# Moving two places for other work in the third layer's attention loop, and two edits around the first layer's experts

## The chip, the cores and the metric

The kernel runs on one core of a Trainium2 chip. The metric is the device time of one execution, in microseconds (us); lower is better. A core has five engines, each with its own queue of instructions that it works off in order: TensorE (matrix products and transposes; PE in the profile, with its weight loads as PEld), VectorE (DVE), ScalarE (ACT), GpSimd (POOL) and SyncE (SP, which issues most of the transfers). They wait for one another by semaphores. TensorE writes its results to PSUM, a small memory of eight banks of 128 x 512 numbers; VectorE and ScalarE read them from there into SBUF, where everything else lies.

## The reference, cut to what matters

The input is x, 8 batches of 512 tokens of 128 numbers. Four layers follow each other, and each is a sandwich: half a feed-forward block, an attention, and the same half feed-forward block again, each on a normalised x:

```python
x = x + 0.5 * _L0_ffn_ref(_layernorm(x), ...)      # 8 experts of capacity 512, top 2; the eighth is a no-op
x = x + _L0_attn_ref(_layernorm(x), ...)           # 16 heads in segments of 32 tokens
x = x + 0.5 * _L0_ffn_ref(_layernorm(x), ...)
x = x + 0.5 * _L1_ffn_ref(...); x = x + _L1_attn_ref(...); x = x + 0.5 * _L1_ffn_ref(...)
x = x + 0.5 * _L2_ffn_ref(...); x = x + _L2_attn_ref(...); x = x + 0.5 * _L2_ffn_ref(...)
x = x + 0.5 * _L3_ffn_ref(...); x = x + _L3_attn_ref(...); x = x + 0.5 * _L3_ffn_ref(...)
```

(The normalisation stands ahead of every block of every layer.) The change touches layer 0's feed-forward blocks and layer 2's attention. The latter, called L2 here, is causal, with 16 heads of 64 and a slope for the distance of two tokens:

```python
q = (x @ Wq).reshape(b, n, H, DH); k = ...; v = ...
scores = einsum('bihd,bjhd->bhij', q, k) * scale + slope * (pos_i - pos_j), masked to j <= i
out = einsum('bhij,bjhd->bihd', softmax(scores), v).reshape(b, n, H * DH) @ Wo + bo
```

The feed-forward block of layer 1 routes a token to one of 64 small splines by two stages of gates (an exponential, a table of knots, a first maximum) and scales a direction by the spline's value. That of layer 2 is one product with a weighted sum of 8 matrices. That of layer 3 adds the products of the 2 best of 8 experts.

## The kernel before, in words

x stays in SBUF, as eight tiles of 128 x 4 x 128 (one a batch). The work runs layer by layer, but a batch's feed-forward blocks of the layers next to an attention are cut into small steps and put between the attention's own work.

**Layer 0's experts** (function `experts`, lines 656 to 710) run twice. A table in DRAM, xd, holds the normalised tokens. For each of seven experts GpSimd gathers 512 rows by four indirect transfers (`fetch`, L664), TensorE turns them (`turn`, L676), multiplies them with the first matrix in four pieces (`inner`, L684, tiles hp), which ScalarE and VectorE take out of PSUM in turn (L688, L686), and with the second (`outer`, L694); ScalarE scales the result (y, L697), and GpSimd writes it out by four indirect transfers (`put`, L668) to a table yd that must hold zeros where no expert writes. There are two such tables, one for each run; `zeros(n)` (L464) fills table n by four transfers of 1 MB from a tile z of zeros. The list `beside` holds small works that are spread over the seven experts, in the place `k * 7 // len(beside)`: in the first run the zeros of the second table, eight `self_part` (the no-op expert's share of a batch, VectorE, L654), and the loads of layer 1's weights. In the second run eight `self_part`, eight `multiply` (the products up x down of layer 3's experts, L1912, in one PSUM bank f3, with loads two ahead, L1905), nine `add` (layer 2's summed matrix, VectorE, L1675; the ninth its bias, L1681) take turns. After each run the rows are read back (L482, tiles r) and added.

**The loop of L2** (lines 1857 to 1891) goes over 64 units, a unit n being a pair of heads of one batch (eight units a batch). The order in which TensorE, ScalarE and VectorE get their instructions is exactly that of the code (`manual_schedule`); GpSimd and SP are ordered by a scheduler. Scores are made in four stretches of queries, i = 0 to 3, of width 128 to 512. `score` (L1753) makes one stretch for both heads of the pair in a PSUM tile s of two banks (two of these tiles); VectorE adds the slopes and finds the minimum in one custom instruction (L1757, the "reduction"); ScalarE takes the exponential (L1760), whose call `score` hands back so that the loop can place it. `norm` (L1787, L1790) divides by the sums. `turn(n, m)` transposes four of the 128 x 128 blocks of the result into one bank (L1779) and hands back ScalarE's copy pt (L1781); five turns, m = 4, 0, 1, 2, 3, make a unit. `project` (L1721, copies qk L1723) makes the queries and keys of a unit, `values` (L1734) half the values of two, `weigh` (L1804, copy att L1807) the weighted values, and `leave` (L1813) the output product of a batch. Turns, projections, values, weighted values and all steps from outside take their PSUM banks from four, tag "mm"; which bank a tile gets is settled when the program is built, by which comes free. In unit n TensorE's order is: three turns of n - 1 (4, 0, 1), the projections of n + 1, scores 2 and 1 of n, turns 2 and 3 of n - 1, values, weighing of n - 2, scores 3 and 0 of n + 1. The exponentials of scores 3 and 0 are kept (`late`) and run at the head of the next unit, between the copies of its first turns.

**The places for other work.** `todo` maps a number to a list of works, and `works(at)` (L1848) runs that list. A unit has three places, 3n, 3n + 1, 3n + 2. In the repeating stretch a batch puts into them, among others:

- layer 2's update: a turned block (L314), then `update` (L348, VectorE L351), in a first and a second place;
- layer 1's front: `scores` and `squeeze` (sp L1048, ScalarE's copy L1049, a gelu L1055 with its table load, VectorE L1054) in a second place, together with an update, and `finish` (VectorE L1060 and L1061, ScalarE's tanh L1063) in the third place after it;
- layer 1's sixteen steps: nearly all on VectorE; `turn` in a first place, `spline` (pa L1138 of 130 columns, ScalarE's copy L1145, eight VectorE steps L1148 to L1155) in the second place, `direct` (pa L1138 of 256 columns, four ScalarE activations L1163 scaled by the spline's result) in the third place after it;
- layer 3's steps: a turned block in a second place, `route` (lp L366, VectorE L416 and L417, ScalarE's exponential L321) in the third place after it, and eight `apply` (yp L384, four VectorE instructions L386) in eight places that follow each other, so in first, second and third ones. The second of the eight shares its place with `direct`.

At the end of the stretch layer 3's first steps come in: a turned block (L314, copy xta L321) in a third place and the first projection (L1979) in a second.

Of the kernel before, what the change touches and what calls it, by code (L numbers as in the profile page):

```python
# [8 lines left out]
F32 = mybir.dt.float32  # L9
# [7 lines left out]
P = 128  # L17
NB = 8
# [126 lines left out]
class Net:  # L145
# [316 lines left out]
        return w  # L462

    def zeros(self, n):  # L464
        for k in range(4):
            self.nc.sync.dma_start(
                out=self.yds[n][2048 * k : 2048 * k + 2048, :].rearrange("(p n) d -> p (n d)", p=P), in_=self.z)
# [24 lines left out]
    def l0_block(self, w):  # L492
# [8 lines left out]
        with ExitStack() as c:  # L501
# [149 lines left out]
            def self_part(b):  # L651
                for i in range(4):
                    t, x = 4 * b + i, self.x[b][:, i, :]
                    nc.vector.scalar_tensor_tensor(x, self.xn[b][:, i, :], box["pw"][:, t, 7:8], x, ALU.mult, ALU.add)  # L654

            def experts(wk, ps, n, beside):

                src, dst, yd = box["src"], box["dst"], self.yds[n]
                gs, gts, hs, ys = {}, {}, {}, {}

                def fetch(e, s):
                    if s == 0:
                        gs[e] = wk.tile([P, 4, P + 8], F32, tag="g", name="g", bufs=4)
                    nc.gpsimd.indirect_dma_start(  # L664
                        out=gs[e][:, s, :], out_offset=None, in_=self.xd[:, :], in_offset=bass.IndirectOffsetOnAxis(ap=src[:, e, s : s + 1], axis=0))

                def put(e, s):
                    put = nc.gpsimd.indirect_dma_start(  # L668
                        out=yd[:, :], out_offset=bass.IndirectOffsetOnAxis(ap=dst[:, e, s : s + 1], axis=0), in_=ys[e][:, s, :], in_offset=None)

                    self.apart(f"puts{n}", put.ins)

                def turn(e):
                    gp = ps.tile([P, 512], F32, tag="mm", name="gp")
                    for s in range(4):
                        nc.tensor.transpose(gp[:, s * P : (s + 1) * P], gs[e][:, s, 0:P], self.ident)  # L676
                    gts[e] = wk.tile([P, 512], F32, tag="gt", name="gt")
                    nc.vector.tensor_copy(gts[e], gp)

                def inner(e):  # L680
                    h = hs[e] = wk.tile([P, 4, 512], F32, tag="h", name="h")
                    for ic in range(4):
                        hp = ps.tile([P, 512], F32, tag="hp", name="hp")
                        nc.tensor.matmul(hp, lhsT=w["w1"][:, e, ic * P : (ic + 1) * P], rhs=gts[e], start=True, stop=True)  # L684
                        if ic % 2:
                            nc.vector.tensor_scalar(h[:, ic, :], hp, 0.0, None, ALU.max)  # L686
                        else:
                            nc.scalar.activation(h[:, ic, :], hp, AF.Relu)  # L688

                def outer(e):  # L690
                    op = ps.tile([P, 4, P], F32, tag="mm", name="op")
                    for s in range(4):
                        for ic in range(4):
                            nc.tensor.matmul(op[:, s, :], lhsT=hs[e][:, ic, s * P : (s + 1) * P], rhs=w["w2"][:, e, ic, :], start=(ic == 0), stop=(ic == 3))  # L694
                    y = ys[e] = wk.tile([P, 4, P], F32, tag="y", name="y", bufs=3)
                    for s in range(4):
                        nc.scalar.activation(y[:, s, :], op[:, s, :], AF.Copy, scale=gs[e][:, s, P + e : P + e + 1])  # L697

                for e in range(3):
                    for s in range(4):  # L700
                        fetch(e, s)
                turn(0)
                for e in range(7):
                    inner(e)
                    if e < 6:
                        turn(e + 1)
                    outer(e)
                    for s in range(4):
                        put(e, s)
                        if e + 3 < 7:  # L710
                            fetch(e + 3, s)
                    for k, work in enumerate(beside):
                        if k * 7 // len(beside) == e:
                            work()
# [171 lines left out]
                slots(bank)  # L886
            with tc.tile_pool(name="f0w", bufs=2) as wk, tc.tile_pool(name="f0e", bufs=2, space=PSUM) as ps, ordered(engines={*FIXED, mybir.EngineType.SP}):
                more = [lambda: box.__setitem__("w1", self.l1_ffn_weights(self.keep))]
                experts(wk, ps, 0, [lambda: self.zeros(1)] + [lambda b=b: self_part(b) for b in range(NB)] + more)
            with tc.tile_pool(name="f0m", bufs=2) as wk, tc.tile_pool(name="f0c", bufs=7, space=PSUM) as ps, ordered(engines=every):  # L890
                todo, bank = {}, banks(ps)
                load, both, add = self.returned(wk, self.yds[0], 3, True)
# [1 line left out]
                for g in range(4):  # L894
                    n = PACE * g
                    for k in range(2):
                        b = 2 * g + k
# [9 lines left out]
            with tc.tile_pool(name="f0w", bufs=2) as wk, tc.tile_pool(name="f0e", bufs=2, space=PSUM) as ps, ordered(engines=FIXED):  # L907
                w2, more = box["w2"]
                w3, steps = self.l3_ffn_weights(self.keep, wk, ps)
                parts = [lambda b=b: self_part(b) for b in range(NB)]  # L910
                experts(wk, ps, 1, [work for works in zip(parts, steps, more(ps)) for work in works] + [more(ps)[8]])
        return box["w1"], w2, w3

    def apart(self, group, ins):
# [774 lines left out]
    def l2_block(self, w1, w2, w3, xt0):  # L1689
# [13 lines left out]
        with ExitStack() as c:  # L1703
            pool = c.enter_context(tc.tile_pool(name="a2", bufs=1))
            wk = c.enter_context(tc.tile_pool(name="a2w", bufs=2))
# [62 lines left out]
            def turn(n, m):  # L1768


                if m == 4:
                    blocks = [(jj, i, 2) for jj in range(2) for i in (2, 3)]
                else:
                    blocks = [(m // 2, i, 1) for i in (1, 2, 3)] + [(m // 2, 3, 3)] if m % 2 else [(m // 2, i, 0) for i in range(4)]
                if n not in turned:
                    turned[n] = wk.tile([P, 5, 512], F32, tag="pt", name="pt")
                tp = bank("tp", (P, 4, P))
                for k, (jj, i, kt) in enumerate(blocks):
                    nc.tensor.transpose(tp[:, k, :], block(n, jj, i, kt), self.ident)  # L1779
                to = turned[n][:, m, :].rearrange("p (k q) -> p k q", q=P)  # L1780
                return lambda: nc.scalar.copy(to, tp)  # L1781
# [35 lines left out]
            last = 8 * NB  # L1817
# [7 lines left out]
            n = 3 * (last - 5)  # L1825
# [21 lines left out]
            def works(at):  # L1847
                for work in todo.pop(at, ()):  # L1848
                    work()
# [4 lines left out]

            late = []
            with tc.manual_schedule(engines={mybir.EngineType.PE, mybir.EngineType.Activation, mybir.EngineType.DVE}):
                for n in range(-4, last + 4):
                    here, prev, two = 0 <= n < last, 1 <= n <= last, 2 <= n <= last + 1
                    if n == -1:
                        run(*project(0))  # L1860
                    outs, qk, exps = [], [], []
                    if prev:
                        outs = [turn(n - 1, m) for m in (4, 0, 1)]
                    if 0 <= n and n + 1 < last:
                        qk = project(n + 1)
                    if here:
                        exps = score(n, 2) + score(n, 1)
                    run(*outs[:2], *late[:2], *outs[2:], *late[2:], *qk, *exps[:2])
                    late = []
                    if prev:  # L1870
                        run(*[turn(n - 1, m) for m in (2, 3)])
                    run(*exps[2:])
                    if here:
                        norm(n, 3, 0)
                    works(3 * n)
                    if here:
                        values(n - n % 2, n % 2)
                    if n >= 3 and (n - 3) % 8 == 7 and n - 3 < last:
                        leave((n - 3) // 8)
                    if two:  # L1880
                        weigh(n - 2)
                    if here:
                        norm(n, 2, 1)
                    works(3 * n + 1)
                    if -1 <= n and n + 1 < last:
                        late = score(n + 1, 3)
                        late += score(n + 1, 0)
                    if -3 <= n < 5:
                        slopes(n + 3)
                    works(3 * n + 2)  # L1890
                assert not todo


# [196 lines left out]
```

## Time and profile before

| what | us |
|---|---|
| median of 3 runs (2604.12 to 2613.46) | 2608.65 |
| the profiled execution's own time | 2601.68 |
| its span | 2599.8 |
| PE busy | 2375.4 (91%) |
| DVE busy | 2019.7 (78%) |
| ACT busy | 1761.3 (68%) |
| POOL busy | 1154.4 (44%) |
| first experts' stage, first gather to last put | 59 to 130 |
| second experts' stage, first gather to last put | 259 to 335 |
| L2's scores, first to last | 987 to 1820 |

Busy time is an average over stages with different limits. In the experts' stages GpSimd issues transfers nearly without a pause; in L2 TensorE is busy nearly all the time. In a row of the groups or of the order of time, the name on the left of the arrow is the tile written, those on the right are read; "[0.53 <-ACT pt L1781]" says that the engine had stood idle for 0.53 us until that instruction released it. "PEld" rows are weight loads, which overlap products.

### The profile page before, as it was taken

The numbers are of one execution on the slowest core, as the hardware profiler recorded it, in microseconds if no ns is written. First come the engines' busy times: TensorE is split into PE (matmuls) and PEld (weight loads), VectorE is DVE, ScalarE is ACT, GpSimd is POOL, SyncE is SP. The second block draws the span as 40 slices with busy tenths as digits, with TensorE's granted clock in tenths as the row PEclk, the third lists the DMA queues.
The fourth block names the chain that finished last, engine by engine and source line by source line (L and its number), as shares of the span: only waits on it lengthen the run. The fifth ranks groups of instructions, "written<-read, shape, count | busy, mean of one in ns | idle before, by whom it ended". The sixth has DMA issues, their size and how long they took to land.

```text
span 2599.8 us, 51330 instructions
## 1 busy us (share of the span) xinstructions
PE 2375.4 (91%) x18184; PEld 1421.3 (55%) x18184; DVE 2019.7 (78%) x5582; ACT 1761.3 (68%) x4413; POOL 1154.4 (44%) x2016
## 2 busy tenths in 40 slices
PE   6868938999999998999999999999899999999997
PEld 6546623344444344565555655656565666666664
DVE  5356368888888847878878787876788989898897
ACT  2244233666677666866767667676688998999996
POOL 5754751444454332264352634432234545454443
PEclk9978957999999999999999999999899999999999
DMA  8221330001010100000000000000000000000000
GB/s 272 59 79 42 107 97 1 19 19 27 20 26 19 35 2 4 1 1 1 1 1 1 1 1 1 1 1 17 1 18 15 5 22 22 10 14 22 22 2 13
DMA packets 72976, 66.51 MB, mean 26 GB/s; under 512 B 15690, under 2 KB 62802, under 8 KB 70578
## 3 DMA queue, kind: packets, MB, share of 16 engines
q1 hardware_dynamic: 68112, 54.88, 7.8%
q0 software_dynamic: 3584, 7.58, 1.1%
q8 instruction: 145, 2.38, 0.4%
q10 hardware_dynamic: 1026, 0.78, 0.1%
q14 instruction: 109, 0.89, 0.1%
HBM read 36.47 MB, written 26.80 MB: 24 GB/s over the span
## 4 chain that ended last, share of the span: by engine, by line
PE 63%; DVE 21%; ACT 8%; POOL 4%; issue 2%; DMA 1%; SPq 0%; ACTq 0%; DVEq 0%; POOLq 0%
PE tp L1477 8%; PE s L1451 6%; PE s L1290 5%; PE o L1804 4%; PE o L1493 4%; PE o L1320 4%; PE s L1753 4%; PE yp L384 3%; PE s L1310 3%; ACT e L1760 3%; DVE nm L1291 3%; DVE nm L1455 3%; PE tp L1779 2%; PE pp L1721 2%; PE hp L684 2%
## 5 line engine op out<-in xcount | busy, mean ns | idle before, releaser
L1462 ACT ACTIVATE e<-s,nm 128x512 f32<-128x512 f32 x512 | 345.0, 688 | 25.9 <-DVE nm L1455 21.4
L1291 DVE TENSOR_REDUCE nm<-s 128x2 f32<-128x1024 f32 x256 | 301.3, 1218 | 75.8 <-PE s L1310 60.9
L1455 DVE TENSOR_REDUCE nm<-s 128x2 f32<-128x1024 f32 x256 | 300.9, 1216 | 29.8 <-PE s L1451 27.8
L1483 ACT ACTIVATE p<-tp 128x512 f32<-128x512 f32 x512 | 278.7, 617 | 63.8 <-PE tp L1477 63.8
L1312 ACT ACTIVATE pr<-s 128x512 f32<-128x512 f32 x512 | 271.5, 601 | 73.1 <-PE s L1310 69.5
L1477 PE MATMUL tp<-cst,e 128*128 128x128 f32 x2048 | 292.8, 281 | 15.2 <-DVE rs L1468 7.9
L1477 PEld LDWEIGHTS tp<-cst,e 128*128 128x128 f32 x2048 | 220.1, 141 | 153.7 <-issue 87.4
L1471 POOL TENSOR_SCALAR e<-e,rs 128x512 f32<-128x512 f32 x113 | 198.3, 1755 | 230.0 <-DVE rs L1468 191.5
L1290 PE MATMUL s<-k,q 32*128 32x512 f32 x1024 | 279.4, 658 | 18.0 <-DVE nm L1291 14.7
L1310 PE MATMUL s<-q,k 32*128 32x512 f32 x1024 | 290.3, 627 | 5.4 <-DVE at L1333 4.3
L1760 ACT ACTIVATE e<-e,m 128x512 f32<-128x512 f32 (+3 forms) x512 | 286.3, 571 | 12.7 <-DVE m L1757 12.5
L1757 DVE CUSTOM_DVE_ANT_0 e<-s,bias 128x512 f32<-128x512 f32 (+3 forms) x512 | 220.1, 486 | 93.2 <-PE s L1753 92.7
L219 POOL TENSOR_TENSOR d<-st 128x4 f32<-128x4 f32 (+3 forms) x90 | 19.5, 217 | 549.4 <-DVE st L215 351.3
L1781 ACT COPY pt<-tp 128x512 f32<-128x512 f32 x320 | 174.4, 589 | 90.3 <-PE tp L1779 90.2
L1471 DVE TENSOR_SCALAR e<-e,rs 128x512 f32<-128x512 f32 x399 | 195.6, 520 | 9.1
L1790 DVE TENSOR_SCALAR e<-e,rc 128x512 f32<-128x512 f32 (+3 forms) x512 | 190.0, 416 | 9.1
L386 DVE SCALAR_TENSOR_TENSOR x<-yp,sel,x 128x128 f32<-128x128 f32 x480 | 166.8, 348 | 32.4 <-PE yp L384 20.9
L1779 PE MATMUL tp<-cst,e 128*128 128x128 f32 x1280 | 171.0, 278 | 9.8 <-ACT pt L1781 4.0
L1451 PE MATMUL s<-k,q 32*128 32x512 f32 x1024 | 174.7, 651 | 5.1 <-ACT e L1462 2.6
L1753 PE MATMUL s<-qk 64*128 64x512 f32 (+3 forms) x1024 | 173.4, 457 | 2.0 <-DVE m L1757 1.3
L1493 PE MATMUL o<-p,va 128*32 128x128 f32 x4096 | 165.8, 277 | 2.9 <-ACT p L1483 2.9
L1779 PEld LDWEIGHTS tp<-cst,e 128*128 128x128 f32 x1280 | 139.2, 141 | 48.5 <-issue 13.6
(476 smaller groups left out, 4844.7 us busy)
## 6 DMA issues: line engine op xcount, KB each, us to landing
yd<-z SPq DMA_DIRECT2D x8, 1024.0 KB
r<-yd SPq DMA_DIRECT2D x32, 256.0 KB
sk<-pu SPq DMA_DIRECT2D x16, 256.0 KB
k<-sk SPq DMA_DIRECT2D x60, 64.0 KB
w<-in_l_w SPq DMA_DIRECT2D x14, 256.0 KB
xd<-wqkv SPq DMA_DIRECT2D x12, 256.0 KB
x<-in_x SPq DMA_DIRECT2D x8, 256.0 KB
up<-in_l_up SPq DMA_DIRECT2D x8, 256.0 KB
```

The costliest lines, as they stand in the source:

```text
L1290: nc.tensor.matmul(s[:, jj, :], lhsT=q[cut, g, i * P : (i + 1) * P], rhs=k[cut, g, :], start=True, stop=True)
L1291: nc.vector.tensor_reduce(nms[b, g // 2][:, i, 2 * h : 2 * h + 2, g % 2], s, AX.X, ALU.max, negate=True)
L1310: nc.tensor.matmul(s, lhsT=k[cut, g, kt * P : (kt + 1) * P], rhs=q[cut, g, :], start=True, stop=True)
L1451: nc.tensor.matmul(s[:, jj, :], lhsT=q[cut, g, i * P : (i + 1) * P], rhs=k[cut, g, :], start=True, stop=True)
L1455: nc.vector.tensor_reduce(nm, scores[n, h], AX.X, ALU.max, negate=True)
L1462: nc.scalar.activation(e, s[:, jj, :], AF.Exp, bias=nm[:, jj : jj + 1], accum_out=sm[:, jj : jj + 1])
L1471: (nc.gpsimd if h and jj and 14 <= n < last - 1 else nc.vector).tensor_scalar(e, e, rc[:, jj : jj + 1], None, ALU.mult)
L1477: nc.tensor.transpose(tp[:, kt, :], probs[n][j][:, kt * P : (kt + 1) * P], self.ident)
L1483: nc.scalar.activation(p, turns[n].pop(0), AF.Exp)
L1753: nc.tensor.matmul(s[:, jj, 0:w], lhsT=qs[n][cut, i * P : (i + 1) * P], rhs=ks[n][cut, 0:w], start=True, stop=True)
L1760: outs.append(lambda e=e, jj=jj: nc.scalar.activation(e, e, AF.Exp, bias=mins[n][:, jj, i : i + 1], scale=-1.0, accum_out=sums[n][:, jj, i ...
L1779: nc.tensor.transpose(tp[:, k, :], block(n, jj, i, kt), self.ident)
```

## The change

It has four parts.

1. `zeros(1)` moves in the first experts' list from the first to the fourth place, behind three `self_part`, and a VectorE memset of one column of z goes ahead of its transfers, so that these wait for VectorE to have come there. The list has ten entries before and after. In SP's order two small loads (gw and sq) now stand ahead of the zeros, and the loads of layer 1's weights behind them, as before.
2. The tiles hp get three buffers for two, in both runs.
3. In the second experts' list `multiply` 5 to 7 and `add` 5 to 8 are taken out and run behind the last expert; the list has 18 entries for 25.
4. In L2's loop `norm(n, 2, 1)` is written ahead of `weigh(n - 2)`; the second place comes behind the scores 3 and 0 of the next unit; and the third place comes in the next unit, behind its first three turns. The loop runs one unit longer for the last third place.

In the built program this gives: ScalarE's and GpSimd's orders in L2 are unchanged. TensorE has second-place work behind scores 3 and 0, and third-place work between the twelve transposes of turns 4, 0, 1 and the projections. VectorE has second-place work behind the reductions of scores 3 and 0. ScalarE's copies of turns 4, 0 and 1 stand behind the ScalarE part of the third place's work, as they did.

```diff
     def zeros(self, n):
+        if n:
+            self.nc.vector.memset(self.z[:, 0:1], 0.0)
         for k in range(4):
...
-                        hp = ps.tile([P, 512], F32, tag="hp", name="hp")
+                        hp = ps.tile([P, 512], F32, tag="hp", name="hp", bufs=3)
...
-                experts(wk, ps, 0, [lambda: self.zeros(1)] + [lambda b=b: self_part(b) for b in range(NB)] + more)
+                experts(wk, ps, 0, [lambda b=b: self_part(b) for b in range(3)] + [lambda: self.zeros(1)] + [lambda b=b: self_part(b) for b in range(3, NB)] + more)
...
-                experts(wk, ps, 1, [work for works in zip(parts, steps, more(ps)) for work in works] + [more(ps)[8]])
+                adds = more(ps)
+                works = [work for works in zip(parts, steps, adds) for work in works[: 3 if works[1] not in steps[5:] else 1]]
+                experts(wk, ps, 1, works)
+                for work in (*steps[5:], *adds[5:]):
+                    work()
...
-                for n in range(-4, last + 4):
+                for n in range(-4, last + 5):
...
                     if prev:
                         outs = [turn(n - 1, m) for m in (4, 0, 1)]
+                    works(3 * n - 1)
                     if 0 <= n and n + 1 < last:
                         qk = project(n + 1)
...
+                    if here:
+                        norm(n, 2, 1)
                     if two:
                         weigh(n - 2)
-                    if here:
-                        norm(n, 2, 1)
-                    works(3 * n + 1)
                     if -1 <= n and n + 1 < last:
                         late = score(n + 1, 3)
                         late += score(n + 1, 0)
+                    works(3 * n + 1)
                     if -3 <= n < 5:
                         slopes(n + 3)
-                    works(3 * n + 2)
```

## Prediction

> **What bounds the kernel now.** I read the page's slices first, then a table by stage, then the waits of TensorE and ScalarE in the second layer (L2), then the order of time around one of its units and around the second experts' stage. The slices say where TensorE is the bound:
>
> ```profile
> PE   6868938999999998999999999999899999999997
> DVE  5356368888888847878878787876788989898897
> ACT  2244233666677666866767667676688998999996
> ```
>
> A digit is a fortieth, 65 us; L2 runs from 986 to 1820 us, slices 15 to 27. One row of the table by stage (busy us of PE, PEld, DVE, ACT, POOL, then the clock):
>
> ```profile
> 1390.00:1490.00 100.00, 94.74 (x561) 58.24 (x561) 79.24 (x307) 67.11 (x187) 45.17 (x102) 1.00 0.00 1
> ```
>
> TensorE is busy 95%, at full clock. So a reordering there can win only the 5% in which it waits, and loses whatever wait it adds. The waits from 986 to 1820 us, TensorE's and ScalarE's (us in all, times, longest):
>
> ```profile
> PE pp L1721 <- ACT pt L1781: 8.8, 6, 2.4
> PE o L1804 <- ACT pt L1781: 6.7, 14, 0.5
> PE tp L1779 <- ACT pt L1781: 4.0, 5, 0.8
> ...
> PE vp L1734 <- ACT pt L1781: 2.5, 4, 0.6
> ```
>
> ```profile
> ACT pt L1781 <- PE tp L1779: 90.2, 43, 3.3
> ...
> ACT pr L321 <- DVE lg L417: 19.8, 7, 3.2
> ACT k L1163 <- PE pa L1138: 16.4, 6, 2.9
> ...
> ACT comp L1063 <- DVE q L1061: 11.7, 6, 2.9
> ```
>
> TensorE's waits end with ScalarE's copies pt of the turned blocks: they free PSUM banks ("mm" has four). The last three ScalarE rows are other work (routing's exponential, the L1 step "direct", the tanh) that stands ahead of those copies in ScalarE's queue and makes it wait. The order of time shows why this costs TensorE little now:
>
> ```profile
> 1408.94 2.37 PE L1804 MATMUL o<-pt,v 128*64 128x512 f32 x16 [0.53 <-ACT pt L1781]
> ...
> 1414.02 1.13 PE L384 MATMUL yp<-wall,xt 128*128 128x512 f32 x2
> ...
> 1414.99 1.03 PE L1138 MATMUL pa<-par,k 128*128 128x256 f32 x4
> ...
> 1415.86 1.03 PE L1779 MATMUL tp<-cst,e 128*128 128x128 f32 x8
> 1416.10 1.14 ACT L1163 ACTIVATE k<-pa,q 128x128 f32<-128x128 f32 x4 [2.88 <-PE pa L1138]
> ...
> 1417.12 1.09 ACT L1781 COPY pt<-tp 128x512 f32<-128x512 f32 x2
> 1417.30 0.66 PE L1779 MATMUL tp<-cst,e 128*128 128x128 f32 x4 [0.41 <-ACT k L1163]
> ```
>
> Product (yp) and table (pa) of the third place run first; TensorE turns blocks while ScalarE finishes the table, and stands for 0.41 us. In the second experts' stage GpSimd is the bound until its last puts wait for y:
>
> ```profile
> 321.80 0.97 POOL L668 DMA_INDIRECT yd<-y,dst  x1 [2.00 <-ACT y L697]
> ...
> 330.34 0.97 POOL L668 DMA_INDIRECT yd<-y,dst  x1 [3.76 <-ACT y L697]
> ...
> 336.73 18.17 SPq L482 DMA_DIRECT2D r<-yd  x16
> ```
>
> **The change, part by part.** Engine by engine in the built program, ScalarE's and GpSimd's orders in L2 are what they were. VectorE does second-place work behind the reductions of scores 3 and 0 instead of ahead of them. TensorE does second-place work behind those scores, and third-place work behind the twelve transposes of blocks 4, 0, 1. Putting norm ahead of weigh moves nothing: they share no engine.
>
> *Third place, the table (direct).* ScalarE copies these transposes only behind the third place's activations, so three of four banks are held and yp and pa must follow each other through the fourth. Take the unit above; weighing ends at 1411.3. TensorE: scores 1.35, yp 1.03, small table 0.5, transposes 1.6, yp 1.03: ready for pa at 1416.9. Its bank is freed by VectorE: reductions start 1.18 after the scores (a unit with idle VectorE: scores 1350.85, reduction 1352.03), at 1412.5, then 1.71 for reductions, 1.50 for the first yp, 1.84 for the eight spline steps, 1.50 for the second yp: 1419.05. Table 1.03, activations 1.14, first copy 0.56: 1421.8. The projections' two banks come from the activations and from that copy; at 0.86 each they end at 1423.2, where scores began at 1419.69. The copies start at 1421.3 instead of 1417.12, ScalarE stays 4.2 late, and the next weighing, which waits for its bank, starts at 1427.85 instead of 1423.72: **+4.1 us**. L1163 counts 24 such activations, 4 each: six units, one without yp (+1.3): 5 x 4.1 + 1.3 = +21.8.
>
> *Second place, update and squeeze.* sp moves behind the scores, 1.35 later, and before its tanh ScalarE has a table load (1.28), gelu (0.31) and VectorE's 0.84 in line: sp copy at 1352.35 for 1351.01, tanh done 1355.9 for 1355.07; copies, and by row "PE pp <- ACT pt" the projections, 0.9 late. Six (L1048 x48, 8 each): +5.4.
>
> *Third place, routing.* From weighing's end at 1387.27, scores 1.35, a turned block 0.55, transposes 1.6, lp 1.06: 1391.85, no longer under the transposes; VectorE's two steps end at 1392.5, and lp's bank is the first projection's: 1392.55 against 1391.51, **+1.0** each; seven (L366 x56): +7.0.
>
> *Third place, products alone.* yp gets the bank of the first copy, done about 1.35 after the transposes start, before they end (1.6): 0. If the copy is late, it costs that lateness; ScalarE idles 3.29 before pt in such a unit. Layer 3's first turned block, moved so in L2's last units, adds its copy's 0.6. Its first query projection, with five DMAs on SP, goes 1.35 later, but the key's, unmoved, follows it, and layer 3 needs both: 0.
>
> *What it gains in L2.* Where yp no longer delays the transposes, copies come 1 us sooner; "PE vp <- ACT pt" should go: -2.5. L2: 21.8 + 5.4 + 7.0 + 0.6 - 2.5 = **+32.3**. Bounds: -22 (all four rows on ACT pt gone), +50 (ScalarE's lateness carried into a second unit each time: 6 x 2.5 more, and the gain absent).
>
> *Second experts' stage.* Two wall products fewer stand ahead of y of expert 6 (0.9, and 1.6 for the pair at 284.88), and a third hp bank takes off 0.45 per expert (block 3.86, four products 3.41), 2.7 for six: y 5.2 earlier. The puts' waits beyond the normal 0.30 are 1.70 and 3.46: 5.16 at most; I take **-4.8**, bounds -5.2 and 0. The three wall products left for the end, with their copies and one load some 7 us, lie under the 11.8 us between that y (329.70 - 5.2) and VectorE's first r (341.12 - 4.8); without that cover the rest of them would be paid. Next late is r<-yd, as now.
>
> *First experts' stage.* GpSimd issues 56 gathers and puts at 1.27 each, from 59.07 to 130.17, never waiting over 1.0: a faster TensorE gives 0. The 4 MB of zeros go from 40 and 54 us to about 91, behind a memset (0.15) that must wait for VectorE; behind it on SP queue ten loads, of which raw is needed first, at 121.30. At 242 GB/s (window 60 to 70) 4 MB end near 108, loads near 112: covered; uncovered, VectorE has 14 us until r at 135.41. Beside zeros the first gather took 6.5 us from issue to TensorE, without them 3.7; GpSimd waits for an issue's landing only eight issues later, 10.2 us: 0, bounds -0.5 (the gathers' first wait) and +6 (a latency doubled to 13, in two rounds of eight). The Trainium skill, "DMA: Bandwidth & Descriptors", section "Issuing engines are not separate DMA queues", says that transfers from all engines share the same 16 engines: that speaks against this move. The rows agree (6.5 against 3.7), but by the rule alone all 17 us of zeros could be paid; with the issue rows, none.
>
> Sum: 32.3 - 4.8 = +27.5 on the profiled 2601.68: 2629.2. That execution is 7.0 under the median of the three runs (2608.65), so in medians **2636**.
>
> The Trainium skill, "Perfetto Trace Analysis", section "Identifying the Most-Contended Engine", holds matmul busy time a bad measure of headroom and puts weight-load time in its place. By that, 58% would leave 42 of 100 us open and a gain far above 22 possible; weighing's 2.30 to 2.38 us in every unit, whatever waits around it, make me keep the 5%.
>
> **The rivals.** *The turned blocks' early start wins* (other side): ScalarE idles 90.2 us before pt; with transposes ahead of third-place work the copies start up to 1 us sooner, and TensorE's 22 us on ACT pt go: 2608.65 - 22 - 4.8 = 2582. For it: those rows. Against: only third places holding products alone let ScalarE past. It decides from where a table unit costs under 1 us instead of 4.1 and routing nothing. 0.12. *L2 doesn't move* (rotation of banks hides both): 2604. Against: three held banks. 0.08. *The lateness carries*: +50 in L2, 2654. For it: units at 1345 to 1363 pass one wait through five rows. 0.06. *Zeros hold up the puts*: +6 on the forecast, 2642. 0.04.
>
> **How the numbers follow.** Forecast 0.70, its own range 2618 to 2650 (table units at 2 to 5.5 us, the others at half to one and a half). All: 2602 to 2660, leaving out the first rival, part of the second and a tail above. A measurement here tells about 0.3%, 8 us: slower is the forecast and its two worse forms, 0.79 after 0.01 of the forecast lost to the band; same is the second rival and that, 0.09; faster 0.12.
>
> **What would show it.** In the profile after: "PE pp <- ACT" or "<- DVE x" grows by 15 us or more and stands behind pa L1144; pt copies behind the table 4 us later after the weighing; VectorE's score wait (91.1) changes little; the last puts of the second stage wait under 0.5; zeros issue near 91 with GpSimd's spacing unchanged. I am wrong if TensorE's share in 1390 to 1490 rises above 95%.

## The result, and the profile after

The kernel after takes 2635.7 us (median of 6 runs, 2629.95 to 2637.14) against 2608.7 us for the kernel before beside it (6 runs, 2604.12 to 2613.46): a ratio of 1.0102, 95% interval 1.009 to 1.0113, or 27 us. Forecast were 2636 us and, in the profiled executions, +27.5. The latter differ by more: 2635.87 against 2601.68, in spans 2634.1 against 2599.8, that is +34.3. By the first and last scores of each layer they part like this: up to layer 1's first score -0.3 (417.0 to 416.7); layer 1's attention, in which no line was changed, +4.8 (519.2 to 524.0); L2's scores, first to last, **+28.7** (833.9 to 862.6); all behind them +1.1. So L2 carries the loss, as forecast, the expected 4.8 from the second experts' stage never arrived, and 4.8 came from a place where nothing was edited.

The slices after, of the page, as before in fortieths of the span:

```profile
PE   6867938999999998999999999999899999999997
DVE  5356377888888838877868787777688989898897
ACT  2244242666676657775766667576598999998996
```

They hardly differ: slices of 66 us hide waits of 2 us. The table by stage shows the loss; its columns are the stretch, then busy us of PE, PEld, DVE, ACT and POOL, then the granted clock. The stretch that had 94.74 us of TensorE before:

```profile
1390.00:1490.00 100.00, 92.21 (x532) 56.06 (x530) 76.87 (x300) 62.42 (x173) 40.86 (x91) 0.96 0.00 1
```

All engines do less in 100 us, and the clock isn't 1.00 any more. TensorE's and ScalarE's waits after, from 970 to 1870 us (us in all, times, longest):

```profile
PE pp L1727 <- ACT pt L1787: 11.7, 6, 2.2
PE pa L1144 <- DVE x L386: 10.7, 5, 2.1
PE o L1810 <- ACT pt L1787: 9.9, 15, 1.0
PE pp L1727 <- ACT k L1169: 8.2, 6, 1.8
PE tp L1785 <- DVE e L1796: 7.1, 9, 1.9
PE pp L1727 <- DVE lg L417: 4.5, 6, 0.8
```

```profile
...
ACT pt L1787 <- PE tp L1785: 68.5, 40, 2.3
ACT k L1169 <- PE pa L1144: 28.8, 5, 6.5
ACT pr L321 <- DVE lg L417: 16.6, 7, 3.9
ACT q L1055 <- PE sp L1054: 16.2, 6, 2.7
...
```

Three rows on TensorE are new: the table pa waits for VectorE to empty yp, and the projections pp wait for the table's activations (k) and for routing (lg). On ScalarE the wait for pa is 12 us longer. The order of time around the table (rows of TensorE, then ScalarE) shows how they hang together:

```profile
1425.11 2.37 PE L1810 MATMUL o<-pt,v 128*64 128x512 f32 x16 [1.00 <-ACT pt L1787]
...
1430.11 1.47 PE L1785 MATMUL tp<-cst,e 128*128 128x128 f32 x12
1431.80 1.12 PE L384 MATMUL yp<-wall,xt 128*128 128x512 f32 x2 [0.23 <-DVE x L386]
1435.07 2.05 PE L1144 MATMUL pa<-par,k 128*128 128x256 f32 x4 [2.14 <-DVE x L386]
1438.39 3.51 PE L1727 MATMUL pp<-xta,wqkv 128*128 128x512 f32 x4 [1.28 <-ACT k L1169]
...
1437.20 1.14 ACT L1169 ACTIVATE k<-pa,q 128x128 f32<-128x128 f32 x4 [6.52 <-PE pa L1144]
1438.21 1.09 ACT L1787 COPY pt<-tp 128x512 f32<-128x512 f32 x2
```

The twelve transposes (1430.11) fill three banks at once, but the copies that free these stand in ScalarE's queue behind the table's four activations (1437.20). yp and pa share the fourth bank, and pa waits for it. ScalarE stands for 6.52 us with finished transposes to copy, and the projections wait for the activations.

Units of a repeating batch, from one weighing's first product to the next one's, in the traces (the kernels in the last four columns are experiments of the next section):

| unit, by what it holds | before | after | third place alone | second place alone | tables back | third place, copies first |
|---|---|---|---|---|---|---|
| products alone | 13.71 | 13.04 | 13.13 | 13.52 | 13.05 | 13.13 |
| update, squeeze, tanh | 16.20 | 16.88 | 16.22 | 16.87 | 16.88 | 14.76 |
| steps on VectorE | 11.02 | 10.93 | 11.02 | 10.94 | 10.93 | 11.02 |
| steps on VectorE | 11.10 | 11.00 | 11.11 | 10.69 | 11.05 | 10.68 |
| routing | 11.94 | 12.48 | 12.44 | 12.47 | 12.48 | 11.42 |
| products alone | 12.10 | 11.42 | 12.09 | 11.43 | 11.42 | 11.88 |
| table | 14.77 | 19.92 | 19.92 | 16.04 | 16.04 | 14.42 |
| output product | 20.05 | 20.01 | 20.15 | 20.31 | 20.04 | 19.85 |

A batch takes 110.9 us before and 115.7 after: the table's unit is 5.15 longer, all others together 0.4 shorter. Over the whole of L2 the six table units are 28.3 us longer (1.66 the one without yp, 5.15 to 5.97 the others), nearly all of its +28.7.

### The profile page after: what moved, and what is told of

Read it like the earlier page. It is cut to its first block, busy times and chain, and to the rows that moved or that the text cites. A ratio compares the mean times of both kernels' runs of the same rounds, so it can differ in the third digit from the quotient of the medians.

```text
span 2634.1 us, 51330 instructions
## 1 busy us (share of the span) xinstructions
PE 2388.6 (91%) x18184; PEld 1433.9 (54%) x18184; DVE 2024.5 (77%) x5583; ACT 1764.3 (67%) x4413; POOL 1152.4 (44%) x2016
## 4 chain that ended last, share of the span: by engine, by line
PE 55%; DVE 20%; ACT 6%; POOL 2%; issue 2%; ACTq 0%; DVEq 0%; POOLq 0%
PE tp L1483 8%; PE s L1457 6%; PE s L1296 5%; PE o L1499 4%; PE o L1326 4%; PE o L1810 4%; PE s L1759 3%; PE s L1316 3%; DVE e L1763 3%; DVE nm L1297 3%; PE yp L384 3%; DVE nm L1461 3%; PE pp L1727 3%; PE tp L1785 2%; PE op L1819 2%; DVE e L1796 2%
## 5 line engine op out<-in xcount | busy, mean ns | idle before, releaser
L1763 DVE CUSTOM_DVE_ANT_0 e<-s,bias 128x512 f32<-128x512 f32 (+3 forms) x512 | 220.2, 485 | 138.1 <-PE s L1759 137.9
L1296 PE MATMUL s<-k,q 32*128 32x512 f32 x1024 | 282.8, 663 | 17.6 <-DVE nm L1297 14.2
L219 POOL TENSOR_TENSOR d<-st 128x4 f32<-128x4 f32 (+3 forms) x90 | 19.5, 217 | 562.0 <-DVE st L215 362.2
```

The lines of the kernel that those rows point to most:

```text
L1296: nc.tensor.matmul(s[:, jj, :], lhsT=q[cut, g, i * P : (i + 1) * P], rhs=k[cut, g, :], start=True, stop=True)
L1763: nc.vector.tensor_tensor_reduce(out=e, in0=s[:, jj, 0:w], in1=bias[:, n % 8 * 2 + jj, 512 - w : 512], scale=1.0, scalar=BIG, op0=ALU.add, ...
```

## The experiments

Each ratio is against the kernel before, run beside it; its time is 2607 us on one of the chips used and 2639 to 2640 on two others, so times of different chips are not to be compared. The column "batch" is a repeating batch in the trace.

| kernel | ratio, 95% | us | L2's scores | batch |
|---|---|---|---|---|
| loop alone | 1.0111 (1.009 to 1.0132) | +29 | 864.2 | 116 |
| third place alone | 1.0122 (1.0094 to 1.015) | +32 | 864.9 | 116.1 |
| second place alone | 1.0032 (1.0015 to 1.0049) | +8 | 846.0 | 112.5 |
| after, copies first | 0.9931 (0.9907 to 0.9954) | -18 | 822.4 | 109 |
| stages alone | 0.9984 (0.9972 to 0.9995) | -4 | 835.6 | 110.9 |
| stages, three load buffers | 0.998 (0.9966 to 0.9994) | -5 | 833.8 | 110.9 |
| after, tables back | 1.0042 (1.0029 to 1.0056) | +11 | 845.0 | 112.4 |
| third place, copies first | 0.9901 (0.9879 to 0.9923) | -26 | 814.4 | 107.2 |
| the same, stages and buffers | 0.9929 (0.9912 to 0.9946) | -19 | 818.0 | 107.2 |
| the same, second place too | 0.9922 (0.9905 to 0.9939) | -21 | 822.5 | 109 |
| exponentials first | 0.992 (0.9897 to 0.9944) | -21 | 817.5 | 108.4 |
| projections first | 0.998 (0.9968 to 0.9993) | -5 | 833.5 | 111 |

**The parts one by one.** The loop of the change alone, in the kernel before:

```diff
...
                     if prev:
                         outs = [turn(n - 1, m) for m in (4, 0, 1)]
+                    works(3 * n - 1)
...
+                    if here:
+                        norm(n, 2, 1)
                     if two:
                         weigh(n - 2)
-                    if here:
-                        norm(n, 2, 1)
-                    works(3 * n + 1)
                     if -1 <= n and n + 1 < last:
                         late = score(n + 1, 3)
                         late += score(n + 1, 0)
+                    works(3 * n + 1)
...
-                    works(3 * n + 2)
```

> The kernel before with the reordered unit of layer 2 alone; the experts' stages stay as before. Theory (the reordering is the whole loss): +25 to +30 us on the kernel before, scores of layer 2 first to last 860 to 865 us (833.9 before). Rival (half of the loss came with the front, by a shifted phase of the clock in layers 1 and 2): +10 to +16 us.

+29 us, and 864.2 us from the first to the last score: the reordering is the whole loss, and the rival, a shifted phase of the clock as the larger cause, falls.

The third place alone:

```diff
...
                         outs = [turn(n - 1, m) for m in (4, 0, 1)]
+                    works(3 * n - 1)
...
-                    works(3 * n + 2)
```

> Only the third place goes behind the first three turned blocks; the second place stays ahead of scores 3 and 0, weighing stays ahead of norm. Theory of the prediction (banks held while ScalarE's copies stand behind the third place's activations): 21.8 + 7.0 + 0.6 - 2.5 = +27 us at most, scaled to the profile's 28.7 for all of it +22 to +25. Rival (VectorE: with the second place behind the scores' reductions its wait for scores grew from 91 to 138 us, so the second place is the loss): +5 us or less.

+32 us with an interval of 25 to 40: more than the theory's +22 to +25, the upper end of which the interval just reaches. The table's unit takes 19.92 us, as it does after. The rival (VectorE's wait for scores is the cause) falls.

The second place alone:

```diff
                     if here:
                         norm(n, 2, 1)
-                    works(3 * n + 1)
                     if -1 <= n and n + 1 < last:
                         late = score(n + 1, 3)
                         late += score(n + 1, 0)
+                    works(3 * n + 1)
```

> Only the second place goes behind scores 3 and 0; the third place stays at the end of the unit, ahead of the next unit's turned blocks. Theory of the prediction: +5.4 us (six tanh units, 0.9 each), and VectorE's wait for scores stays near 91 us. Rival (VectorE idles for scores while the second place's work waits behind them): +20 us or more and the wait near 138 us.

+8 us (4 to 13): the theory's 5.4 lies inside. VectorE's wait for scores grew to 129.4 us all the same, so that row tells little about a cause: VectorE stands for scores whenever TensorE is late. What costs most here had been expected of another unit. The tanh unit takes 0.67 more (forecast 0.9); the table's unit takes 1.27 more, since the small table, now behind the scores, brings the factors for direct later. In the order of time (ScalarE, then TensorE):

```profile
1345.37 1.14 ACT L1163 ACTIVATE k<-pa,q 128x128 f32<-128x128 f32 x4 [2.95 <-DVE q L1155]
...
1346.56 0.66 PE L1779 MATMUL tp<-cst,e 128*128 128x128 f32 x4 [1.96 <-ACT k L1163]
```

ScalarE waits for VectorE's last step of the spline, and the third transposed block for the bank that ScalarE then frees. When both places move, this lies inside the table's larger loss, and the routing unit, which takes 0.5 more with either place alone, takes the 0.5 only once: the two edits alone add up to 40 us, together they cost 29.

**Is it the place of the copies in ScalarE's queue?** TensorE's and VectorE's orders stay those of after; only ScalarE's copies pt go ahead of the third place's ScalarE work (the exponentials of scores 3 and 0, which were woven between them, stay behind it):

```diff
+                    run(*outs)
                     works(3 * n - 1)
...
-                    run(*outs[:2], *late[:2], *outs[2:], *late[2:], *qk, *exps[:2])
+                    run(*late, *qk, *exps[:2])
```

> The kernel after, but ScalarE's copies of the three turned blocks stand ahead of the third place's ScalarE work in its queue; TensorE's and VectorE's orders stay those of after. Theory of the prediction (the copies' place in ScalarE's queue holds the banks): the table and routing terms, 21.8 + 7.0, go, and the time is -20 to -28 us against after, so -3 to +7 us against before. Rival (TensorE's own order, or VectorE's, makes the loss): within 8 us of after, +19 to +27. Rival (dips of the granted clock make it): in between, with the dips still there, +10 to +18.

-18 us against before, so by the two ratios some 45 less than after takes: the whole loss is gone, and there is a gain instead, as the first rival of the prediction had it. TensorE's waits of pa for VectorE and of pp for k and lg are no longer among its rows. TensorE's order alone isn't the cause, then, and the clock's dips, which were expected to leave +10 to +18, aren't by themselves either. The size was missed: the theory gave back the loss alone.

The same with the second place left ahead of the scores, and the experts' stages as before:

> The kernel before with only the third place moved behind the first three turned blocks and ScalarE's copies of these put ahead of the place's ScalarE work; the second place stays ahead of scores 3 and 0, and the experts' stages stay as before. If the copies' place is all that made the third place's move a loss: -12 to -20 against before. Rival (the gain of the full version needs the second place behind the scores as well): 0 to -6.

```diff
                         outs = [turn(n - 1, m) for m in (4, 0, 1)]
+                    run(*outs)
+                    works(3 * n - 1)
...
-                    run(*outs[:2], *late[:2], *outs[2:], *late[2:], *qk, *exps[:2])
+                    run(*late, *qk, *exps[:2])
...
-                    works(3 * n + 2)
```

2583.4 us against 2607.2: a ratio of 0.9901, the largest gain of all and one that beats both kernels. It is 26 us (20 to 32), more than the 12 to 20 expected. The order of time around the table (TensorE, then ScalarE):

```profile
1411.35 1.53 PE L1779 MATMUL tp<-cst,e 128*128 128x128 f32 x12
1412.71 1.02 PE L384 MATMUL yp<-wall,xt 128*128 128x512 f32 x2
1413.57 1.03 PE L1138 MATMUL pa<-par,k 128*128 128x256 f32 x4
1414.44 1.88 PE L1721 MATMUL pp<-xta,wqkv 128*128 128x512 f32 x4
...
1412.09 1.56 ACT L1781 COPY pt<-tp 128x512 f32<-128x512 f32 x3 [1.55 <-PE tp L1779]
1414.69 1.14 ACT L1163 ACTIVATE k<-pa,q 128x128 f32<-128x128 f32 x4 [1.03 <-PE pa L1138]
```

The copies run under yp and pa, pa has a bank of its own, and TensorE doesn't stop between the transposes and the projections. The table's unit falls to 14.42 us, that of the update to 14.76; with 1.44 less a batch the latter is the largest part of the gain.

**How much is the table?** After, with the third places of the six table units back at the end of their unit:

```diff
-                    works(3 * n - 1)
+                    if n - 1 not in range(8, 49, 8):
+                        works(3 * n - 1)
...
+                    if n in range(8, 49, 8):
+                        works(3 * n + 2)
```

> The kernel after with the third place of the six table units (direct, and the products beside it) back at the end of the unit, ahead of the next unit's turned blocks; every other third place stays behind them. By the prediction's terms 21.8 us of 32.3 go: -20 to -24 against after, +3 to +7 against before. Rival (the loss is spread over routing, update and table units alike): -8 or less, +19 or more against before.

+11 us (8 to 15) against before: 16 us, not 21.8, go with the tables, by the difference to after's 27. The trace has L2 17.6 us shorter than after's. The table is the largest part, but its unit keeps the 1.27 of the second place, which the prediction had counted into the table's 4.1. What is left of the loss in the trace, 845.0 - 833.9 = 11.1 us, is close to the prediction's other terms in L2 (5.4 + 7.0 + 0.6 - 2.5 = 10.5) by chance only: the six table units hold 9.7 of it (1.67, four times 1.26 or 1.27, and 2.96), and all other units together little more than 1.

**The experts' stages alone** (the first three parts of the change, in the kernel before):

```diff
+            self.nc.vector.memset(self.z[:, 0:1], 0.0)
...
+                        hp = ps.tile([P, 512], F32, tag="hp", name="hp", bufs=3)
...
+                works = [work for works in zip(parts, steps, adds) for work in works[: 3 if works[1] not in steps[5:] else 1]]
+                experts(wk, ps, 1, works)
+                for work in (*steps[5:], *adds[5:]):
+                    work()
```

> The kernel before with the three edits of the experts' stages alone (zeros later, a third hp bank, the shorter list with three products, three tables' sums and the bias at the end); layer 2 stays as before. Theory formed on the traces (the puts end 3.8 us sooner, but the read r of the second stage waits for the left-over products and the bias): -0.3 us, at most -1.5. Rival (the prediction): -4.8 us.

The time is 4 us less (1 to 7), which is nearer to the rival, the prediction's -4.8. The trace doesn't show where: r is issued 0.8 us sooner, layer 1's first score comes at 416.5 for 417.0. In the kernel after, the second stage reads:

```profile
326.52 0.97 POOL L670 DMA_INDIRECT yd<-y,dst  x1 [0.70 <-ACT y L699]
...
330.34 0.96 POOL L670 DMA_INDIRECT yd<-y,dst  x1 [0.30 <-issue]
```

```profile
332.21 2.04 PE L1918 MATMUL pp<-down,up 128*128 128x128 f32 x8 [3.82 <-DMA down<-in_l_down]
334.62 0.79 PE L1687 MATMUL bp<-gb,wb 8*128 8x128 f32 x2 [0.37 <-ACT wall L1919]
```

```profile
SPq L484 <- DMA yd<-y,dst: 4.6, 1, 4.6
SPq L484 <- PE bp L1687: 2.6, 1, 2.6
```

The last put comes 3.82 us sooner (330.34 for 334.16), yet r (L484) waits 2.6 us longer on SP's queue, for the last left-over work, the bias bp. That comes late because the last wall product waits 3.82 us for its load, which is issued two products ahead and so only behind product 5, at the stage's end. A third buffer for up and down issues it one product sooner:

```diff
-                t = got[e, name] = wk.tile([P, 4, P], F32, tag=name, name=name)
+                t = got[e, name] = wk.tile([P, 4, P], F32, tag=name, name=name, bufs=3)
...
-            if e + 2 < 8:
-                load(e + 2)
+            if e + 3 < 8:
+                load(e + 3)
```

> The same as the experts' stages' edits alone, with a third buffer for the tiles up and down, so that their last load is issued one product sooner and the left-over products don't wait for it (3.82 us in the profile after). If r waits for those products, r is issued 2 to 3.5 us sooner and the time is -2 to -3.5 us against the edits alone. Rival (r waits for the puts' landing or for the queue, whatever the products do): 0.

Read r now waits for the landing of the puts alone, and bp is long done:

```profile
329.19 0.48 PE L1687 MATMUL bp<-gb,wb 8*128 8x128 f32 x2 [0.37 <-ACT wall L1919]
```

```profile
331.93 6.28 SPq L484 DMA_DIRECT2D r<-yd  x9
```

r is issued 2.69 us behind the last put for 5.27, and layer 1's first score comes at 412.3: 4.8 us before that of the kernel before. The medians differ by 3.6 us, about the theory's upper end (2 to 3.5), but the intervals of the two kernels overlap, so the gain in time isn't shown.

**Joining, and two more orders.** The stages with the third buffer, the third place with copies first, and on top of it the second place, or the exponentials of scores 3 and 0 between the copies ahead of the third place, or the projections and their copies ahead of it:

> Three things joined: the experts' stages of the new kernel with the third buffer for up and down, the third place behind the first three turned blocks, and ScalarE's copies of these ahead of the place's work; the second place stays ahead of the scores. If the parts add: 0.9901 x 0.998 of before, that is -24 - 5 = -29 us. If they hide each other: -24 or less.

> The same, with the second place behind scores 3 and 0 as in the change. Theory (a small table that comes later makes the activations of direct later, whichever order the copies have; blocks of 108.9 us against 107.2): +8 to +11 us against the version with the second place ahead of the scores. Rival (the difference was the chip's, and the second place costs only where the turned blocks wait for it): 0 to +3.

```diff
...
+                    run(*outs[:2], *late[:2], *outs[2:], *late[2:])
+                    works(3 * n - 1)
...
-                    run(*outs[:2], *late[:2], *outs[2:], *late[2:], *qk, *exps[:2])
+                    run(*qk, *exps[:2])
```

> The version with the second place ahead of the scores, with the four exponentials of scores 3 and 0 ahead of the third place's ScalarE work too, as they were woven between the copies before. If the exponentials' lateness holds up norm and the transposes (TensorE's 4.2 us of waits for VectorE's e): -1 to -4 us. If the third place's activations come too late for their bank instead: +2 to +6.

```diff
+                    run(*outs)
                     if 0 <= n and n + 1 < last:
                         qk = project(n + 1)
+                    run(*qk)
+                    works(3 * n - 1)
...
-                    run(*outs[:2], *late[:2], *outs[2:], *late[2:], *qk, *exps[:2])
+                    run(*late, *exps[:2])
```

> The version with the second place ahead of the scores, with the next unit's projections and their copies ahead of the third place. TensorE's waits of 9.1 us for ScalarE's copies of projections, ahead of whiten's transposes, should go: -5 to -9 us. Rival (the scores then wait longer, or the projections wait for the banks of the turned blocks' copies): 0 or more.

Joined, the gain is 19 us (14 to 23), not the sum of 29. This ran on one of the slower chips; the experts' stages were not measured by themselves there, so it stays open whether their 4 us exist on it. The second place behind the scores changes nothing in the time (0.9922 against 0.9929, where 8 to 11 us had been expected and 0 to 3 was the rival), though the trace has 109 us a batch against 107.2; that profiled execution was also 7.7 us above its median, and I leave this open. Exponentials first can't be told from it either, so it is the copies' place that counts and not what is woven between them. Projections first loses most of the gain, some 14 us: the turned blocks' later copies then hold up the weighing, by the waits of TensorE from 1020 to 1900 us (the first row is 6.8 us in the joined kernel without this edit):

```profile
PE o L1810 <- ACT pt L1787: 26.4, 20, 2.7
PE tp L1785 <- DVE e L1796: 9.0, 13, 1.9
```

The waits for ScalarE's copies of projections, which it was to remove, are gone; a larger one took their place.

## Why the prediction was right, and where it wasn't

The direction, the mechanism and the place were right: in the built order three banks are held by transposes whose copies stand behind the third place's ScalarE work. That the total hit to within a us is partly luck: +28.7 for +32.3 in L2, about nothing for -4.8 in the second stage's trace, and 4.8 from layer 1, which no term had, make +34.3 in the profiled executions. L2's own sum is luck in part, too: the six table units took 28.3 us for a forecast of 21.8, and all the rest of L2, forecast at +10.5, about 0.4. The prediction raised its sum by the 7.0 by which the profiled execution before lay under its median; that of after lies at its median, and so +34.3 there is +27.0 in medians.

- **Table, +4.1 a unit.** Right in its steps: moved by the 16.2 us between the weighings, pa was forecast for 1435.2 and starts at 1435.07. Measured are +5.15, of them 3.2 in waits (19.92 - 16.28 for 14.77 - 14.36) and 1.9 in longer busy time (16.28 for 14.36), in a unit whose clock is 0.91 for 1.00. The lateness was a little oversized, and the clock, which the term had left at full speed, more than made up for it.
- **Second place, +0.9 a unit:** 0.67 in four of the six tanh units, but nothing in another and -0.65 in the first: 2.0 in all for 5.4. By itself it costs the table's unit 1.27 too, through the spline's factors; the term for the table had this in its chain.
- **Routing, +1.0 a unit:** 0.52 to 0.54 in five of the seven units, 0.89 and 1.32 in the last two: 4.9 in all for 7.0. Mis-sized; the wait for lg is 0.8 at the longest.
- **Products alone 0, and vp's wait -2.5 in all:** both such units gain 0.67, 1.3 a batch where 0.4 was expected. In the first of them this comes with the third place (13.13 in that alone), so the gain from an earlier start was undersized; in the second it comes with the second place (11.43 in that alone, 12.09 with the third place alone), which the prediction had at nothing. Why the second place gives it stays open.
- **"VectorE's score wait (91.1) changes little":** wrong. It is 137.9 us. TensorE's lateness turns up on every engine that waits for scores; I had looked for it on ScalarE alone.
- **First experts' stage, 0:** right. The zeros are issued at 89.8, r at 131.6 as before, and the first gather at 59.0.
- **Second experts' stage, -4.8:** y did come early (the last puts 3.8 sooner, with a wait of 0.70 where under 0.5 was forecast), but the step "The three wall products left for the end ... lie under the 11.8 us" failed. The cover was measured on VectorE, up to its first r. The read r itself is issued earlier and stands on SP behind the bias, and the last load is issued later because its product moved. Both stand in the order of SP's queue, which the prediction had named for the first stage and left out for this one. With the third buffer the 4.8 us are there in the trace.
- **The first rival, the early start of the turned blocks (2582 us):** not in this change, but the experiments made it true. With the copies ahead, a table unit costs -0.35 us, under the 1 us from which the prediction let it win, and the kernel takes 2583.4. That this is so near 2582 is partly chance: the 2582 held 4.8 us from the second experts' stage, which this kernel leaves as it was.
- **The 5% to win:** the bound of 22 us held (the best order gained 19.5 in L2), but not because TensorE's idle time is all that there is to win. A batch of before, of after, and of the third place with copies first:

```profile
1325.75:1436.66 110.91, 105.50 (x625) 64.56 (x624) 89.52 (x348) 75.94 (x213) 49.13 (x110) 1.00 0.00 1
```

```profile
1342.08:1458.66 116.58, 108.17 (x623) 66.55 (x622) 90.27 (x348) 76.47 (x213) 48.73 (x110) 0.96 0.00 1
```

```profile
1326.10:1433.30 107.20, 103.68 (x624) 64.66 (x624) 89.38 (x348) 76.54 (x213) 49.55 (x110) 1.00 0.00 1
```

With the same products (623 to 625 of them in the records) TensorE is busy for 105.50, 108.17 and 103.68 us, and idle for 5.4, 8.4 and 3.5. Of the 3.7 us gained by the last one, 1.8 came out of "busy" time at the same clock. A busy share is no floor. The Trainium skill, "Perfetto Trace Analysis", section "Identifying the Most-Contended Engine", which holds matmul busy time a bad measure, agrees with these three rows in that; one of the measures that it puts in its place, weight-load time (64.66 of 107.20 us here), leaves far more open than any order found.

## What to carry to other kernels

When work is moved ahead on one engine, follow who frees its buffers on the others: transposes that start sooner hold their banks until their copies' turn comes in ScalarE's queue, so move the copies with them. One line of ScalarE's order was worth 45 us here, more than the change itself. Where steps are pushed behind a stage "because there is time", look at what waits for them and at the loads that they issue, on the queue that issues the next stage's reads.

## What the hardware did that I had not expected

Short waits cost twice. In the kernel after, L2's clock falls to half in every batch (6.8 us, in one batch 10.2, of 116); before, one stretch of 3.4 us was all. Around the table, in steps of 3.4 us:

```profile
1427.90:1431.30 3.40, 3.40 (x25) 2.52 (x22) 2.92 (x13) 0.59 (x2) 0.00 (x0) 1.00 0.00 0
1431.30:1434.70 3.40, 1.40 (x5) 0.34 (x3) 3.05 (x14) 0.00 (x0) 0.00 (x0) 1.00 0.00 0
1434.70:1438.10 3.40, 2.05 (x4) 1.18 (x4) 0.22 (x1) 0.90 (x4) 0.00 (x0) 0.50 0.00 0
1438.10:1441.50 3.40, 3.11 (x4) 1.18 (x4) 0.00 (x0) 3.40 (x11) 1.27 (x1) 0.50 0.00 0
1441.50:1444.90 3.40, 3.40 (x19) 2.00 (x19) 2.06 (x10) 2.94 (x10) 0.00 (x0) 1.00 0.00 0
```

A stretch in which TensorE worked 1.40 of 3.40 us is followed by two at clock 0.50, in the first of which it again worked only 2.05; the four projections took 3.51 us for 1.97 before. Two table units of this kernel differ in the clock alone:

```profile
1309.39:1329.31 19.92, 16.28 (x74) 8.54 (x74) 11.86 (x49) 10.82 (x32) 1.26 (x1) 0.91 0.00 1
1425.11:1445.86 20.75, 17.10 (x74) 9.13 (x74) 11.87 (x49) 10.84 (x32) 1.27 (x1) 0.84 0.00 1
```

A clock of 0.91 over 19.92 us is 3.6 us at half, 0.84 over 20.75 us is 6.6: one such stretch more, with the same idle time (3.64 and 3.65 us), cost 0.8. The Trainium skill, "TensorE: Matmul & The Clock Gate", section "What's actually happening", says that the clock is halved after at least one idle window of about 3.4 us. The length agrees with these stretches, but no window here was idle: the longest wait in this one is 2.14 us. The measurement decides: a window that is 41% busy is enough. It is so from 1137 to 1670 us as well: in the windows of 3.40 us just ahead of the ten stretches at half, TensorE was busy for 1.13 to 1.51 us.

The same gate moves time about where no code was changed. Layer 1's attention took 518.2 to 526.1 us in the traces of all these kernels; 524.0 in the trace of after, at a mean clock of 0.95 from 417 to 941 us, and 519.2 in that of before, at 0.96. The clock's records have it at half for 47.8 us there after and for 37.5 before; half of the difference is 5.1 us, and the times differ by 4.8. A difference of 5 us between two single executions is thus no evidence for an edit elsewhere.

Two of the three chips that ran experiments needed 30 us more for the kernel before. In the traces from there the time is lost ahead of layer 1: with the experts' stages of before, the last put came at 362.2 us for 334.2 and layer 1's first score at 444.8 for 417.0. The reason stays open.
